# Run sums kept in PSUM, the weighted sum moved into a branch, and the rest of an FFN spread over the next attention

## The chip, the cores and the metric

The kernel is one program on one core of a Trainium2 chip. The core has TensorE (PE, with its weight loads listed as PEld), VectorE (DVE), ScalarE (ACT), GpSimd (POOL) and the DMA queues, of which SP and ACT issue plain transfers and POOL issues gathers by index. The metric is the device time of one execution in microseconds. The kernel before ran at a median of 6830.59 us over three runs (6827.94 to 6841.34).

## The reference

Four layers work on 6250 nodes with 256 features each, and each adds its result to `x`:

```python
x = x + gat(layernorm(x), src, dst, W, att_src, att_dst, bias)          # 4 heads of 64, 206,250 edges
x = x + moe(layernorm(x)[None], ...)                                     # 8 experts, the best 2 of each node
x = x + weighted_gnn(layernorm(x), src, dst, edge_weight, W1, b1, W2, b2)
x = x + gat_moe(layernorm(x)[None], ..., edge_index)                     # 4 heads of 4, routes to 4 experts
```

The change is about the third and the fourth. In the third, with `emb = layernorm(x)`:

```python
messages = edge_val[:, None] * embeddings[edge_src]
neighbor_emb = segment_sum(messages, edge_dst, n_nodes)
side_emb = (neighbor_emb + neighbor_emb * embeddings) @ W2.T + b2
out = leaky_relu(embeddings @ W1.T + b1 + side_emb, 0.2)
return out / max(norm(out), 1e-12)
```

In the fourth, an attention over a second list of 131,072 edges (its nodes are drawn from 0 to 8191, and those from 6250 on belong to no node here) gives every node a score for each of four experts; the best two weigh two of the four dense networks `gelu(x @ W1[e] + b1[e]) @ W2[e] + b2[e]`, which all run on all nodes.

## The kernel before

Nodes lie on 128 partitions in 49 blocks; `X` holds the features of all of them in SBUF throughout. An edge list sorted by target is cut into tiles of 128 edges, one edge a partition, and eight tiles (`Q = 8`) make a piece. One gather instruction of POOL fetches the 128 rows of one tile by a column of indices.

The stages follow each other: first attention (`gat_stream`, lines 1155 to 1388, over 1612 gathers), the FFN with eight experts (`routed_ffn`, loop from line 590), weighted sum (lines 1884 to 2033), second attention (`layer1_fast` at line 1685, which calls `gat_stream` again). Outside `tc.manual_schedule()` a planner orders the instructions of each engine; inside, they stay as written. The weighted sum's loop and both `gat_stream` loops are written out by hand.

Beside the first FFN run two generators, advanced four steps a tile of 256 rows (`next(beside, None)`): `sorted_edges` sorts the second edge list and checks it, `runs_of` (line 1524) prepares the weighted sum's indices `si_d`, weights `wab_d` and places `dab_d`. `runs_of` goes through two chunks of 128 pieces; its `turned` makes two times four transposes on PE, each set of four evicted by ScalarE.

The weighted sum first normalises `X` into a table in DRAM, `tab_ef` (lines 1885 to 1889), and then steps over 202 pieces. The edges of a piece lie in such a way that a partition holds eight consecutive edges, which belong to one target or two: two runs. `wab` has two weights for each edge, one for each run, of which one is zero. Step `s_` does, in this order:

- eight gathers for piece `s_` into `g1` (five buffers), line 234
- one piece of the second FFN's work, if there is any (`beside`)
- four matmuls `acc` for piece `s_ - 3` (line 2011), which add the run sums to their targets by one-hot matrices `oh`; after two pieces ScalarE takes the sum out (`kept`)
- another piece of FFN work
- the side steps of a finished block, one a step: `move` (shift to a block, PE), `side` (two transposes of two halves, with ScalarE's evictions between), `dense` (PE, then VectorE's `on`), `norm` (ScalarE and VectorE), `next_ln` (VectorE), `next_h` (transposes, then a small matmul and VectorE's `h`)
- `sum_runs(s_ - 2)`: ScalarE writes the first product of each run into SBUF, VectorE adds the 13 others (line 1922), and one instruction makes both one-hots from `ips`, a list of 0 to 127 in PSUM (line 1924)
- a third piece of FFN work

All engines take their instructions in order. `next_h` stores the second attention's rows to DRAM (`tab_1`, read by its gathers, and `ha_d`), and every four blocks it starts a group of the second FFN (`dense_ffn`, line 1616): pieces of eight matmuls into two PSUM buffers `pf`, each followed by a gelu or a copy on ScalarE and a store of `y1` to `y_d`. What is left of it when the loop ends runs in `while beside(): pass`. Then the program reads a flag that says whether the second list is in order, branches, and `layer1_fast` loads `si1`, `HN` (from `ha_d`), `dl1`, `il1` and starts its gathers; its step has five calls of its own `beside`, which do the weighted additions `put` (line 1756). The other branch sorts in a general way and isn't taken with these inputs.

PSUM has eight banks of 128 x 512 floats. The weighted sum uses all: `acc1` 2, `bacc1` 2, `pt` 1, `ips` 1, `pf` 2.

Of the kernel before, what the change touches and what calls it, by code (L numbers as in the profile page):

```python
# [20 lines left out]
F32 = mybir.dt.float32  # L21
BF = mybir.dt.bfloat16
I32 = mybir.dt.int32
# [9 lines left out]
P = 128  # L33
# [38 lines left out]
def tile_kernel(ctx, tc, src_ins, out):  # L72
# [1447 lines left out]
    def runs_of(s, sp, pp, si, wab, dab):  # L1520
# [19 lines left out]
        def turned(dst, src):  # L1540
            d, t = (a.rearrange("p (r j) -> p r j", j=Q) for a in (dst, src))
            for j0 in range(0, Q, 4):
                pt = pp.tile([P, 4, P], F32, name="pt_s")
                for j in range(4):
                    nc.tensor.transpose(pt[:, j], t[:, :, j0 + j], ident)
                nc.scalar.copy(d[:, :, j0:j0 + 4].rearrange("p r j -> p j r"), pt)

        for c in range(-(-npiece // P)):
# [4 lines left out]
            nc.vector.tensor_copy(b, a.bitcast(I32))  # L1553
            nc.vector.tensor_scalar(x, b, 0.0, float(N), op0=OP.is_lt, op1=OP.mult)
            nc.vector.tensor_add(b, b, x)
            nc.vector.tensor_scalar(b, b, 0.0, float(N - 1), op0=OP.max, op1=OP.min)
            yield
            y = room("B1")
            turned(y, b)
# [10 lines left out]
            turned(d, b)  # L1570
            yield
            load(w, I["edge_weight"], c, nr)
            wt = room("A0")
            turned(wt, w)
            yield
            d3 = d.rearrange("p (r j) -> p r j", j=Q)
            first = d3[:, :, 0:1].to_broadcast([P, P, Q])
            for k, op in enumerate((OP.is_equal, OP.not_equal)):
                m = room(("A1", "B1")[k])
                nc.vector.tensor_tensor(m.rearrange("p (r j) -> p r j", j=Q), d3, first, op=op)  # L1580
                nc.vector.tensor_mul(m, m, wt)
# [103 lines left out]
    def layer1_fast(s1, si1, dl1, il1, ha_d, tab_1, y_d):  # L1685
# [3 lines left out]
        with tc.tile_pool(name="g1f", bufs=1) as g1, tc.tile_pool(name="f1w", bufs=2) as fp:  # L1689
            si = g1.tile([P, s1.C * P], I32, name="si1s")  # L1690
            nc.sync.dma_start(si, si1)
            HN = g1.tile([P, NT, W1 + H1], F32, name="HN")
            nc.sync.dma_start(HN, ha_d)
# [75 lines left out]
            def beside():  # L1769
                if work:  # L1770
                    work.pop(0)()
                return bool(work)
# [5 lines left out]
    def fast(flag_s0, last_d, dl_d):  # L1778
# [104 lines left out]
        ha_d = dram.tile([P, NT, D1 + 2 * H1], F32, name="ha_d")  # L1883
        y_d = dram.tile([NT, P, C1, D], F32, name="y_d")
        with tc.tile_pool(name="n1e", bufs=2) as mp:
            for t0, n in chunks(NT, CH):
                em = mp.tile([P, CH, D], F32, name="em")
                layernorm(mp, em, X[:, t0:t0 + n, :], n)
                nc.sync.dma_start(tab_e[t0 * P:(t0 + n) * P].rearrange("(t p) d -> p t d", p=P), em[:, :n])
        with tc.tile_pool(name="n1f", bufs=1) as ep, tc.tile_pool(name="n1fw", bufs=2) as mp, \  # L1890
                tc.tile_pool(name="n1f_ps", bufs=1, space=PSUM) as pp, \
                tc.tile_pool(name="f1_ps", bufs=2, space=PSUM) as fpp:
            si = ep.tile([P, npiece * Q], I32, name="si8")
            nc.sync.dma_start(si, si_d)
            wab = ep.tile([P, 2, npiece * Q], F32, name="wab")
            nc.sync.dma_start(wab, wab_d.rearrange("k p t -> p k t"))
            dab = ep.tile([P, npiece * 2], F32, name="dab")
            nc.sync.dma_start(dab, dab_d)
            w12 = ep.tile([P, 2, KD, D], F32, name="w12")
            nc.sync.dma_start(w12[:, 0], I["L1_gnn_W1"].rearrange("(k p) f -> p k f", p=P))  # L1900
            nc.sync.dma_start(w12[:, 1], I["L1_gnn_W2"].rearrange("(k p) f -> p k f", p=P))
            bb = ep.tile([P, 2, D], F32, name="bb12")
            nc.sync.dma_start(bb[:, 0], rows(I["L1_gnn_b1"]))
            nc.sync.dma_start(bb[:, 1], rows(I["L1_gnn_b2"]))
            bias = ep.tile([P, D], F32, name="bias12")
            nc.vector.tensor_add(bias, bb[:, 0], bb[:, 1])
            wg = layer1_weights(ep)
            room, start, beside = dense_ffn(ep, mp, fpp, y_d)
            ips = place_iota(pp)
            acc, piece, runs, ems, sums_of = {}, {}, {}, {}, {}  # L1910

            def sum_runs(q):

                g = piece.pop(q)
                r = [mp.tile([P, D], F32, name=f"run{i}", bufs=3) for i in range(2)]
                for j in range(Q):
                    for i in range(min(2, j + 1)):
                        w = wab[:, i, q * Q + j:q * Q + j + 1]
                        if j == i:
                            nc.scalar.activation(r[i], g[:, j, :], AF.Copy, scale=w)  # L1920
                        else:
                            nc.vector.scalar_tensor_tensor(r[i], g[:, j, :], w, r[i], op0=OP.mult, op1=OP.add)  # L1922
                oh = mp.tile([P, 2, P], F32, name="oh", bufs=3)
                nc.vector.tensor_tensor(oh, ips[:, None, :P].to_broadcast([P, 2, P]),  # L1924
                                        dab[:, 2 * q:2 * q + 2, None].to_broadcast([P, 2, P]), op=OP.is_equal)
                runs[q] = r, oh

            def move(i, kept):

                whole = []  # L1930
                for b in range(NT):
                    of = s0.parts_of(b)
                    if i in of:
                        if b not in sums_of:
                            sums_of[b] = pp.tile([P, D], F32, name="bacc1", bufs=2)
                            ems[b] = mp.tile([P, D], F32, name="emb", bufs=3)
                            nc.sync.dma_start(ems[b], tab_e[b * P:(b + 1) * P])
                        nc.tensor.matmul(sums_of[b], shift_to(s0, i, b), kept, start=(i == of[0]), stop=(i == of[-1]))
                        if i == of[-1]:
                            whole.append(b)  # L1940
                return whole

            def side(b):
                sd = mp.tile([P, D], F32, name="sd_", bufs=2)
                nc.vector.scalar_tensor_tensor(sd, ems[b], 1.0, sums_of.pop(b), op0=OP.add, op1=OP.mult)
                eT = mp.tile([P, KD, P], F32, name="eT")
                transposed(pp, eT, ems.pop(b))
                sT = mp.tile([P, KD, P], F32, name="sT")
                transposed(pp, sT, sd)
                return eT, sT  # L1950

            def dense(b, eT, sT):
                po = pp.tile([P, KD, P], F32, name="pt").rearrange("p k e -> p (k e)")
                for k in range(KD):
                    nc.tensor.matmul(po, eT[:, k], w12[:, 0, k], start=(k == 0), stop=False)
                for k in range(KD):
                    nc.tensor.matmul(po, sT[:, k], w12[:, 1, k], start=False, stop=(k == KD - 1))
                o = mp.tile([P, D], F32, name="on")
                nc.vector.tensor_add(o, po, bias)
                nc.vector.scalar_tensor_tensor(o, o, 0.2, o, op0=OP.mult, op1=OP.max)  # L1960
                return o

            def norm(b, o):
                sq = mp.tile([P, D], F32, name="sq", bufs=1)
                ss = mp.tile([P, 1], F32, name="ss")
                nc.scalar.activation(sq, o, AF.Square, accum_out=ss)
                nc.scalar.activation(ss, ss, AF.Sqrt)
                nc.vector.tensor_scalar_max(ss, ss, 1e-12)
                nc.vector.reciprocal(ss, ss)
                nc.vector.scalar_tensor_tensor(X[:, b, :], o, ss, X[:, b, :], op0=OP.mult, op1=OP.add)  # L1970

            def next_ln(b):
                xl = mp.tile([P, 1, D], F32, name="xl1")
                layernorm(mp, xl, X[:, b:b + 1, :], 1)
                return xl

            def next_h(b, xl):
                o = b % GB * P
                xT = room(b // GB)[:, :, o:o + P]
                transposed(pp, xT, xl[:, 0, :])  # L1980
                ph = pp.tile([P, KD, P], F32, name="pt")[:, 0, :D1 + 2 * H1]
                for k in range(KD):
                    nc.tensor.matmul(ph, xT[:, k], wg[:, k], start=(k == 0), stop=(k == KD - 1))
                h = mp.tile([P, D1 + 2 * H1], F32, name="h1")
                nc.vector.tensor_copy(h, ph)
                nc.sync.dma_start(tab_1[b * P:(b + 1) * P], h[:, :D1 + H1])
                nc.sync.dma_start(ha_d[:, b, :], h)
                if b % GB == GB - 1 or b == NT - 1:
                    start(b // GB)

            chain = {side: dense, dense: norm, norm: next_ln, next_ln: next_h}


# [89 lines left out]
```

## Time and profile before

| what | us |
| --- | --- |
| median of three runs | 6830.59 |
| the profiled execution | 6821.2 |
| its span in the profile | 6819.3 |
| first attention, first to last gather | about 190 to 2240 |
| FFN with eight experts and its sum | about 2400 to 3400 |
| weighted sum, first to last gather | 3442 to 5623 |
| second attention, from its first gather | 5730 to 6819 |
| POOL busy | 4252.7 |
| VectorE busy | 4025.0 |
| TensorE busy | 3924.9 |
| ScalarE busy | 1166.6 |

A row of the groups names line, engine, operation and tile, then the count, the busy time in us, the mean of one in ns, and the engine's idle time just before these instructions with what ended it. A row in order of time has the start, the duration, the engine and, in brackets, how long the engine was idle before and for whom. A row of a stretch has its limits and length, then the busy time of PE, PEld, VectorE, ScalarE and POOL, PE's granted clock, the DMA share and GB/s.

### The profile page before, as it was taken

The numbers are of one execution on the slowest core, as the hardware profiler recorded it, in microseconds if no ns is written. First come the engines' busy times: TensorE is split into PE (matmuls) and PEld (weight loads), VectorE is DVE, ScalarE is ACT, GpSimd is POOL, SyncE is SP. The second block draws the span as 40 slices with busy tenths as digits, with TensorE's granted clock in tenths as the row PEclk, the third lists the DMA queues.
The fourth block names the chain that finished last, engine by engine and source line by source line (L and its number), as shares of the span: only waits on it lengthen the run. The fifth ranks groups of instructions, "written<-read, shape, count | busy, mean of one in ns | idle before, by whom it ended". The sixth has DMA issues, their size and how long they took to land.

```text
span 6819.3 us, 61938 instructions
## 1 busy us (share of the span) xinstructions
PE 3924.9 (58%) x17463; PEld 2934.8 (43%) x17463; DVE 4025.0 (59%) x9984; ACT 1166.6 (17%) x2834; POOL 4252.7 (62%) x4320
## 2 busy tenths in 40 slices
PE   4466665666666579998624566666666665111111
PEld 3344444444444468886513444444444443111111
DVE  5455555555555872443356565555566651788888
ACT  2000000000000112232112233323333332000000
POOL 0777777777777012332167777777777772777774
PEclk9677777777777589998856787778787887555555
DMA  4545555545554145556543444444444441223222
GB/s 135 139 137 139 138 138 139 138 138 138 138 137 128 45 128 194 186 185 206 163 152 105 110 115 113 112 112 113 112 114 114 113 113 53 64 66 66 68 66 56
DMA packets 502756, 822.99 MB, mean 121 GB/s; under 512 B 149744, under 2 KB 321987, under 8 KB 502370
## 3 DMA queue, kind: packets, MB, share of 16 engines
q0 software_dynamic: 190880, 462.26, 25.6%
q1 hardware_dynamic: 298854, 345.00, 16.5%
q10 hardware_dynamic: 12668, 11.68, 0.6%
q8 instruction: 141, 2.31, 0.1%
q14 instruction: 213, 1.74, 0.1%
HBM read 743.88 MB, written 77.89 MB: 121 GB/s over the span
## 4 chain that ended last, share of the span: by engine, by line
PE 26%; DVE 22%; POOL 19%; issue 15%; DMA 13%; ACT 4%; DVEq 0%; SPq 0%; another core or an unknown queue 0%; POOLq 0%; ACTq 0%
POOL g L1214 15%; DVE run L1922 7%; DMA g<-tab,si 7%; PE ph L601 5%; PE py L614 4%; POOL g L234 4%; PE acc L2011 4%; PE acc L1316 3%; PE pf L1654 2%; DMA g<-tab_1f,si1s 2%; DVE X L1756 2%; PE pf L1665 2%; DMA g<-tab_ef,si 2%; DVE g L1293 1%; PE pt L263 1%
## 5 line engine op out<-in xcount | busy, mean ns | idle before, releaser
L234 POOL DMA_INDIRECT g<-tab_ef,si x1616 | 1688.6, 1045 | 591.0 <-issue 437.0
L1214 POOL DMA_INDIRECT g<-tab,si x1612 | 1540.8, 956 | 494.3 <-issue 408.9
L1316 PE MATMUL acc<-g,oh 128*128 128x264 f32 x3224 | 1042.5, 488 | 338.8 <-DVE g L1293 333.9
L1922 DVE SCALAR_TENSOR_TENSOR run<-g,wab,run 128x256 f32<-128x256 f32 x2626 | 1088.8, 478 | 98.9 <-DMA g<-tab_ef,si 65.7
L1316 PEld LDWEIGHTS acc<-g,oh 128*128 128x128 f32 x3224 | 772.0, 247 | 560.4 <-DVE g L1293 394.5
L1214 POOL DMA_INDIRECT g<-tab_1f,si1s x787 | 770.1, 979 | 247.8 <-issue 213.3
L2011 PE MATMUL acc<-run,oh 128*128 128x256 f32 x808 | 336.9, 559 | 857.5 <-DVE oh L1924 857.2
L2011 PEld LDWEIGHTS acc<-run,oh 128*128 128x128 f32 x808 | 195.0, 265 | 993.4 <-DVE oh L1924 834.6
L1246 DVE TENSOR_TENSOR z<-g,nd 128x32 f32<-128x32 f32 (+1 forms) x301 | 57.7, 192 | 752.3 <-DMA g<-tab,si 654.2
L1293 DVE TENSOR_TENSOR g<-g,pe 128x2048 f32<-128x2048 f32 (+2 forms) x301 | 486.8, 1617 | 0.0
L1316 PE MATMUL acc<-s,oh 128*128 128x72 bf16 x1267 | 96.7, 251 | 601.4 <-DVE s L1298 601.4
L1654 PE MATMUL pf<-xt,w 128*128 128x512 f32 (+1 forms) x832 | 424.6, 650 | 1.5 <-ACT h L1659 1.0
L1665 PE MATMUL pf<-w,h 128*128 128x256 f32 x1568 | 413.9, 417 | 12.6 <-ACT h L1659 12.6
L601 PE MATMUL ph<-xe,w 128*128 128x256 f32 x1792 | 404.7, 382 | 0.0
L614 PE MATMUL py<-w,h 128*128 128x256 f32 x1792 | 400.7, 381 | 0.0
L577 POOL DMA_INDIRECT xg<-tab_x,gi x112 | 123.2, 1100 | 408.1 <-PE pt L586 322.4
L1665 PEld LDWEIGHTS pf<-w,h 128*128 128x128 f32 x1568 | 333.7, 214 | 86.8 <-ACT h L1659 17.5
L601 PEld LDWEIGHTS ph<-xe,w 128*128 128x128 f32 x1792 | 341.3, 192 | 45.6
L614 PEld LDWEIGHTS py<-w,h 128*128 128x128 f32 x1792 | 337.2, 191 | 43.3
L1316 PEld LDWEIGHTS <-oh 128*128 128x128 bf16 x1267 | 90.2, 134 | 605.2 <-issue 500.8
L1235 PEld LDWEIGHTS <-ot 128*128 128x128 bf16 x2879 | 116.1, 102 | 457.7 <-DVE ot L1224 403.3
L617 POOL DMA_INDIRECT tab_y<-y,so x112 | 118.6, 1059 | 296.6 <-DVE y L616 292.4
(486 smaller groups left out, 5689.4 us busy)
## 6 DMA issues: line engine op xcount, KB each, us to landing
w<-in_L_ffn_W SPq DMA_DIRECT2D x112, 1024.0 KB
db<-s_d SPq DMA_DIRECT2D x299, 256.0 KB
g<-tab_ef,si POOLq DMA_INDIRECT x1616
g<-tab,si POOLq DMA_INDIRECT x1612
y_d<-y SPq DMA_DIRECT2D x196, 128.0 KB
yb<-y_d SPq DMA_DIRECT2D x49, 512.0 KB
g<-tab_1f,si1s POOLq DMA_INDIRECT x787
yy<-tab_y SPq DMA_DIRECT2D x7, 1792.0 KB
```

The lines of the kernel that those rows point to most:

```text
L234: nc.gpsimd.indirect_dma_start(out=dst, out_offset=None, in_=table, in_offset=bass.IndirectOffsetOnAxis(ap=si[:, t:t + 1], axis=0))
L577: nc.gpsimd.indirect_dma_start(out=xg[:, i, :], out_offset=None, in_=tab_x, in_offset=bass.IndirectOffsetOnAxis(ap=gi[:, 2 * j + i:2 * j + ...
L601: nc.tensor.matmul(ph, w1[:, k, f * P:(f + 1) * P], xe[:, k, :], start=(k == 0), stop=(k == KD - 1))
L614: nc.tensor.matmul(py, hs[f][:, i * P:(i + 1) * P], w2[:, f, :], start=(f == 0), stop=(f == FC - 1))
L1214: nc.gpsimd.indirect_dma_start(out=g[:, j, :DH + H], out_offset=None, in_=tab, in_offset=bass.IndirectOffsetOnAxis(ap=si[:, t0 + j:t0 + j ...
L1293: nc.vector.tensor_mul(gh, gh, ps[i][:, o:o + n, :, None].to_broadcast([P, n, H, CD]))
L1316: nc.tensor.matmul(acc[b].rearrange("p s w -> p (s w)"), oh[:, t - a], m_, start=(t == lo), stop=(t == hi))
L1654: nc.tensor.matmul(ph[:, :n], w1[:, e, k, f * P:(f + 1) * P], xts[g][:, k, :n], start=(k == 0), stop=(k == KD - 1))
L1665: nc.tensor.matmul(py[:, :D], hs[g, e, f][:, j * P:(j + 1) * P], w2[:, e, f, :], start=(f == 0), stop=(f == FC - 1))
L1756: nc.vector.scalar_tensor_tensor(X[:, b, :], v[:, e, :], gates[:, j, e:e + 1], X[:, b, :], op0=OP.mult, op1=OP.add)
L1922: nc.vector.scalar_tensor_tensor(r[i], g[:, j, :], w, r[i], op0=OP.mult, op1=OP.add)
L2011: nc.tensor.matmul(acc[i], oh[:, k], r[k], start=(q % 2 == 0 and k == 0), stop=(last and k == 1))
```

## The change

Four things are changed.

- `sum_runs` keeps both run sums of a piece in one PSUM bank, `at`, until the last term, which goes to SBUF. The first product of the first run is made by VectorE, that of the second run still by ScalarE. The one-hots come from `iota` in SBUF, an instruction each, since `ips` gives its bank to `at`. `run` and `kept1` have two buffers for three.
- The weighted sum becomes a function that runs inside the branch on the second list's flag. `HN` is a tile in SBUF that `next_h` fills, `ha_d` goes, and `si1` and the FFN's weights are loaded at the start of the branch.
- `while beside(): pass` goes. What is left of the second FFN runs in the second attention's calls of `beside`, ahead of the additions.
- `runs_of` has more yields: after each instruction over a whole chunk and after each set of four transposes.

```diff
@@ runs_of
                     nc.tensor.transpose(pt[:, j], t[:, :, j0 + j], ident)
                 nc.scalar.copy(d[:, :, j0:j0 + 4].rearrange("p r j -> p j r"), pt)
+                yield
...
             nc.vector.tensor_copy(b, a.bitcast(I32))
+            yield
             nc.vector.tensor_scalar(x, b, 0.0, float(N), op0=OP.is_lt, op1=OP.mult)
+            yield
             nc.vector.tensor_add(b, b, x)
+            yield
             nc.vector.tensor_scalar(b, b, 0.0, float(N - 1), op0=OP.max, op1=OP.min)
             yield
             y = room("B1")
-            turned(y, b)
+            yield from turned(y, b)
...
-            turned(d, b)
-            yield
+            yield from turned(d, b)
             load(w, I["edge_weight"], c, nr)
             wt = room("A0")
-            turned(wt, w)
-            yield
+            yield from turned(wt, w)
...
                 nc.vector.tensor_tensor(m.rearrange("p (r j) -> p r j", j=Q), d3, first, op=op)
+                yield
                 nc.vector.tensor_mul(m, m, wt)
@@ layer1_fast
-    def layer1_fast(s1, si1, dl1, il1, ha_d, tab_1, y_d):
+    def layer1_fast(s1, si, dl1, il1, HN, tab_1, y_d, rest):
...
-            si = g1.tile([P, s1.C * P], I32, name="si1s")
-            nc.sync.dma_start(si, si1)
-            HN = g1.tile([P, NT, W1 + H1], F32, name="HN")
-            nc.sync.dma_start(HN, ha_d)
...
             def beside():
-                if work:
+                if not rest() and work:
                     work.pop(0)()
                 return bool(work)
@@ sum_runs
-                r = [mp.tile([P, D], F32, name=f"run{i}", bufs=3) for i in range(2)]
+                    at = pp.tile([P, 2, D], F32, name="run")
+                    r = [mp.tile([P, D], F32, name=f"run{i}", bufs=2) for i in range(2)]
                 for j in range(Q):
                     for i in range(min(2, j + 1)):
                         w = wab[:, i, q * Q + j:q * Q + j + 1]
-                        if j == i:
-                            nc.scalar.activation(r[i], g[:, j, :], AF.Copy, scale=w)
-                        else:
-                            nc.vector.scalar_tensor_tensor(r[i], g[:, j, :], w, r[i], op0=OP.mult, op1=OP.add)
+                            if j == 0:
+                                nc.vector.tensor_scalar(at[:, i], g[:, j, :], w, None, op0=OP.mult)
+                            elif j == i:
+                                nc.scalar.activation(at[:, i], g[:, j, :], AF.Copy, scale=w)
+                            else:
+                                nc.vector.scalar_tensor_tensor(at[:, i] if j < Q - 1 else r[i], g[:, j, :], w, at[:, i],
+                                                               op0=OP.mult, op1=OP.add)
                 oh = mp.tile([P, 2, P], F32, name="oh", bufs=3)
-                nc.vector.tensor_tensor(oh, ips[:, None, :P].to_broadcast([P, 2, P]),
-                                        dab[:, 2 * q:2 * q + 2, None].to_broadcast([P, 2, P]), op=OP.is_equal)
+                    for i in range(2):
+                        nc.vector.tensor_scalar(oh[:, i], iota, dab[:, 2 * q + i:2 * q + i + 1], None, op0=OP.is_equal)
@@ next_h
-                h = mp.tile([P, D1 + 2 * H1], F32, name="h1")
-                nc.vector.tensor_copy(h, ph)
-                nc.sync.dma_start(tab_1[b * P:(b + 1) * P], h[:, :D1 + H1])
-                nc.sync.dma_start(ha_d[:, b, :], h)
+                    nc.vector.tensor_copy(HN[:, b, :], ph)
+                    nc.sync.dma_start(tab_1[b * P:(b + 1) * P], HN[:, b, :D1 + H1])
@@ after the loop over pieces, and the branch
-                while beside():
-                    pass
...
+        def with_ffn(then):
+            with tc.tile_pool(name="f1e", bufs=1) as ep, tc.tile_pool(name="f1o", bufs=2) as fp, \
+                    tc.tile_pool(name="f1_ps", bufs=2, space=PSUM) as fpp:
+                HN = ep.tile([P, NT, D1 + 2 * H1], F32, name="HN")
+                si = ep.tile([P, C1s * P], I32, name="si1s")
+                nc.sync.dma_start(si, si1)
+                room, start, beside = dense_ffn(ep, fp, fpp, y_d)
+                weighted_sum(room, start, beside, HN)
+                then(si, HN, beside)
...
         with tc.If(v1 == 1) as cmp1:
-            layer1_fast(s1, si1, dl1, il1, ha_d, tab_1, y_d)
+            with_ffn(lambda si, HN, rest: layer1_fast(s1, si, dl1, il1, HN, tab_1, y_d, rest))
```

## The prediction

> **What bounds the kernel now.** I read the groups first, then the waits, then the rows in order of time. The bound of a change is about 0.2% (14 us): less can't be told from none.
>
> The groups give the weighted sum's gathers, its run sums and its matmuls:
>
> ```profile
> L234 POOL DMA_INDIRECT g<-tab_ef,si x1616 | 1688.6, 1045 | 591.0 <-issue 437.0
> L1214 POOL DMA_INDIRECT g<-tab,si x1612 | 1540.8, 956 | 494.3 <-issue 408.9
> L1922 DVE SCALAR_TENSOR_TENSOR run<-g,wab,run 128x256 f32<-128x256 f32 x2626 | 1088.8, 478 | 98.9 <-DMA g<-tab_ef,si 65.7
> L2011 PE MATMUL acc<-run,oh 128*128 128x256 f32 x808 | 336.9, 559 | 857.5 <-DVE oh L1924 857.2
> ```
>
> POOL's idle time is 98.9 us before the first gather and 0.30 us before every other: it never waits for a buffer, so gathers set this stage (1688.6 + 492 = 2181 us). A gather here takes 1045 ns; over the first attention, the same instruction takes 956. The rows in order of time show where the difference comes from:
>
> ```profile
> 4499.84 4.03 DVE L1922 SCALAR_TENSOR_TENSOR run<-g,wab,run 128x256 f32<-128x256 f32 x10
> ...
> 4501.83 1.28 POOL L234 DMA_INDIRECT g<-tab_ef,si  x1 [0.30 <-issue]
> ...
> 4505.00 0.95 POOL L234 DMA_INDIRECT g<-tab_ef,si  x1 [0.30 <-issue]
> ```
>
> Beside the run sums (two SBUF inputs: a row of `g` and `run`) a gather can take 1.28 us; once they are over, 0.95. Now the consumer, VectorE, over one block:
>
> ```profile
> 4066.34 0.42 DVE L1924 TENSOR_TENSOR oh<-ips,dab 128x256 f32<-128x256 f32 x1
> ...
> 4073.17 0.18 DVE L1985 COPY h<-pt 128x24 f32<-128x24 f32 x1 [6.08 <-PE pt L1983]
> 4073.26 5.35 DVE L1922 SCALAR_TENSOR_TENSOR run<-g,wab,run 128x256 f32<-128x256 f32 x13
> 4078.54 0.41 DVE L1924 TENSOR_TENSOR oh<-ips,dab 128x256 f32<-128x256 f32 x1
> 4084.48 0.42 DVE L1959 TENSOR_TENSOR on<-pt,bias 128x256 f32<-128x256 f32 x1 [5.53 <-PE pt L1957]
> ...
> 4090.55 0.41 DVE L1924 TENSOR_TENSOR oh<-ips,dab 128x256 f32<-128x256 f32 x1
> ...
> 4109.23 0.41 DVE L1924 TENSOR_TENSOR oh<-ips,dab 128x256 f32<-128x256 f32 x1
> ```
>
> Four pieces, that is about one block of 128 nodes, in 42.9 us, and no row among them waits for a gather; a piece takes 10.7 though its run sums take 5.35, because VectorE waits for PE in between. The loop is serial: run sums, one-hots, PE's `acc`, FFN and side matmuls, VectorE's side step, next run sums. Over the stage the first one-hot starts at 3473.2 and the last at 5626.83: 2153.6 us, 10.71 a piece. VectorE's waits for gathers (65.7 directly, 25.8 through ScalarE's run; 93.1 by the rows) are all the slack: without them the consumer needs 2060.5 us. **Two chains within 5% of each other**: whoever shortens one by lengthening the other must sum both.
>
> **1. Run sums in PSUM: the gathers.** With `at` in PSUM an instruction has one SBUF tensor left. The row for that is the first attention, whose big multiply reads `pe` from PSUM: 956 ns. So 1616 x (956 + 304) = 2036 us, 145 less. The other end is no gain at all (2181), if the operand is not the cause.
>
> **2. Run sums in PSUM: the consumer.** Per piece:
> - Term j = 0 moves from ScalarE to VectorE, 478 ns by L1922's row, and the next instruction reads its result; dependent rows (L1756 in the second attention) start 0.52 us apart, independent ones 0.40. Plus 0.52.
> - Second run's first product stays on ScalarE, now in the same PSUM bank as the first run. Halves of one bank are handed over one by one in this trace, though the halves are disjoint:
>
> ```profile
> 3342.28 0.27 ACT L1094 COPY ips<-iota 128x128 f32<-128x128 f32 x1 [6.88 <-DVE y L616]
> 3342.58 0.29 DVE L1095 TENSOR_SCALAR ips<-iota 128x128 f32<-128x128 f32 x1 [0.39 <-ACT ips L1094]
> ...
> 1000.57 0.20 ACT L1285 ACTIVATE g<-zt 128x32 f32<-128x32 f32 x1 [0.26 <-DVE g L1286]
> 1000.80 0.19 DVE L1286 TENSOR_TENSOR g<-zt,il 128x32 f32<-128x32 f32 x1 [0.26 <-ACT g L1285]
> ```
>
>  So VectorE's second instruction ends, ScalarE starts 0.03 later, takes 0.49 (L1920: 491 to 498 ns; evictions of this size take 0.37, a lower end), VectorE resumes 0.03 later; the old dependent gap of 0.04 falls away: plus 0.51. Its other end is 0, if it isn't handed over. Behind ScalarE's wait stand gelu and the `y` copies; PE's `pf` buffers need them, but PE idles 857 us for the one-hots (the group of `acc`) and can take that.
> - One-hots: two tensor_scalar from SBUF (L549: 279 ns each, 0.08 overlapped) for one of 413: plus 0.07.
> - 13 other instructions: a PSUM operand costs nothing by the rows (L1959 reads PSUM, 424 ns; L1860 reads SBUF, 424); the destination neither (L1095 into PSUM, 0.29). I take 0. The upper end is that neighbours in one bank also wait for each other, 0.52 for 0.40 on 11 of them: plus 1.3. A lower end below 0 is nothing I can place: L1945, with PSUM input and no pointer, is 0.02 shorter than L1861; 13 x 0.02 = 0.3 us a piece.
>
>  Sum 1.10 us; 201 x 1.10 = 221; the consumer needs 2282 and is the bound, 128 more than 2153.6. What is late next: gathers, now waiting for g's five buffers. Smaller buffer counts (`run`, `kept1`: 2) cost nothing: their readers are one step behind.
>
> [...]
>
> **3. FFN's rest beside the second attention.** Between the last one-hot (5626.83) and the next gather (5730.40) lie 103.6 us, 61 of them FFN alone:
>
> ```profile
> 5662.00:5723.00 61.00, 60.34 (x261) 44.87 (x259) 0.00 (x0) 20.19 (x46) 0.18 (x1) 1.00 0.13 42
> ...
> 5730.40 0.96 POOL L1214 DMA_INDIRECT g<-tab_1f,si1s  x1 [7.39 <-DMA vec<-in_L_ffn_ln_gamma]
> ```
>
> `si1` and HN are then in SBUF already (their loads, 5.4 us, and the 49 stores to `ha_d` on SP go). The last `tab_1` store is issued at 5661.4; with some 3 us to land and 3 of setup the first gather starts near 5667: minus 63. About 50 FFN items move into the first 10 steps, 5 a step. PE has 19% to do there; 5 x 1.7 = 8.5 us a step fit in a piece of 10.2. At half clock they are 17, a lag that nine g buffers take for three steps. I take plus 5, range 0 to 30. SP's `db` loads queue behind `y_d` stores that wait for ScalarE; they are issued two steps ahead, which covers it.
>
> **4. Weighted sum inside the branch.** The branch itself is about 1 us (flag at 65.62, SP's next load at 66.70). The layernorm can no longer fill VectorE's gaps in the sum over experts before it: two chunks, 7 us. ScalarE's queue gets the FFN's weight loads ahead of the layernorm's roots; these held it from 3436.4 to 3456.2. SP gets one `si1` load. Plus 15 (7 to 25).
>
> **5. More yields in the list's preparation.** In the first FFN, bound by PE, tiles of 14.25 us stretch to as much as 38 while transposes wait (12.4 us for the casts, 9.4 for edge weights), about 50 us in all. The steps now spread over 8.5 tiles in place of 4, with 4.5 tiles left. The wait for edge weights stays in one step. Minus 20 (0 to 40).
>
> **Sum.** 6821.2 (span 6819.3 and 1.9 around it; the median of the runs is 6830.6, 0.14% above) + 128 - 63 + 5 + 15 - 20 = **6886 us**.
>
> **Rivals.**
> - *The handover is hidden* (faster): ScalarE writes while VectorE adds. Consumer +0.59: 2179, +26; with -63 for the rest 6784. It decides at 0.78 us a piece (93 + 63 over 201). For: the halves are disjoint. Against: both pairs of rows above.
> - *Sum no longer than before* (faster): gathers and consumer meet at 2061: -93 - 63 = 6665. [...] Against: VectorE has an instruction more.
> - *Neighbours in one bank wait* (slower): +2.4 us a piece, 2543: 7147.
> - *The gathers don't get shorter*: 2181 stays under 2282, so nothing changes in mine; in the second rival it leaves the stage at 2181 and the whole at 6821 - 63 = 6758.
>
> **Numbers.** Mine 0.46, hidden handover 0.24, no longer sum 0.14, neighbours wait 0.11, others 0.05. The side terms spread mine by about 40 us, so of its 0.46 some 0.38 are slower, 0.04 same, 0.04 faster; the hidden handover gives 0.22 faster and 0.02 same, the third rival 0.11 slower, the others 0.04 slower and 0.01 faster. Range 6645 to 7010: it leaves out the waiting neighbours and some of the others. Slower 0.53, same 0.06, faster 0.41.
>
> **What would show it.** Right: gathers near 0.96 with POOL waiting for run sums; ScalarE's run idle behind VectorE, VectorE behind ScalarE, in every piece; one-hots 11.3 us apart; first gather of the second attention 40 us after the last one-hot. Wrong: POOL still without waits and one-hots 10.2 apart.

## The result, and the profile after

The changed kernel takes 7086.2 us in the median of four runs (7082.1 to 7091.4). Against the kernel before that is a ratio of 1.0372, with a 95% interval of 1.0354 to 1.0390. The prediction said 6886 and 6645 to 7010: the sign was right, the size was not, and the time lies outside the range. The experiments below were measured in four later sets of runs, each with the kernel before beside it, whose median was 7995, 6864, 7913 and 6849 us in turn; every ratio is to the kernel before of the same set.

The profiled execution has a span of 7089.6 us. Cut at the same events as the span before, it shows where the time came from:

| stretch | before | after | difference | predicted |
| --- | --- | --- | --- | --- |
| start to the start of the last `y` of the first FFN (yields) | 3341.8 | 3328.4 | -13.4 | -20 |
| from there to the first gather of the weighted sum (branch, start) | 100.5 | 112.0 | +11.5 | +15 |
| first gather to the end of the last one-hot (weighted sum) | 2184.9 | 2523.7 | +338.8 | +128 |
| from there to the first gather of the second attention | 103.2 | 37.7 | -65.5 | -63 |
| second attention | 1088.9 | 1087.8 | -1.1 | +5 |

Four of the five rows lie within 7 us of their terms; the whole miss is the weighted sum. The groups of the kernel after (busy time in us and mean of one in ns, then idle time just before and what ended most of it):

```profile
L234 POOL DMA_INDIRECT g<-tab_ef,si x1616 | 1528.7, 946 | 1054.8 <-issue 1022.2
L1214 POOL DMA_INDIRECT g<-tab,si x1612 | 1542.1, 957 | 494.1 <-issue 411.6
L1923 DVE SCALAR_TENSOR_TENSOR run<-g,wab,run 128x256 f32<-128x256 f32 x2626 | 1264.7, 488 | 211.7 <-ACT run L1921 111.8
L2011 PE MATMUL acc<-run,oh 128*128 128x256 f32 x808 | 337.0, 559 | 1102.7 <-DVE oh L1927 1102.7
```

The gathers did get shorter, 1045 to 946 ns, as forecast. But POOL's idle time rose from 591 to 1055 us. Of that, 0.30 us before each gather (485 us) is there in both kernels, and 110 us stand before the first gather (99 in the kernel before). The other 460 us or so are waits for a free buffer `g`, which the profile puts down as "issue": they come before the first gather of a piece, and in 125 pieces that gather starts about 0.74 us after the last addition that reads the buffer it is to fill. One of VectorE's additions is only 10 ns longer (478 to 488), yet together they are busy for 176 us more (1264.7 to 1088.8): they overlap less. The rows of VectorE and ScalarE in order of time, over one step:

```profile
4514.82 0.18 DVE L1986 COPY HN<-pt 128x24 f32<-128x24 f32 x1 [5.59 <-PE pt L1985]
4514.92 0.48 DVE L1919 TENSOR_SCALAR run<-g,wab 128x256 f32<-128x256 f32 x1
4515.43 0.49 DVE L1923 SCALAR_TENSOR_TENSOR run<-g,wab,run 128x256 f32<-128x256 f32 x1
4515.95 0.48 ACT L1921 ACTIVATE run<-g,wab 128x256 f32<-128x256 f32 x1 [2.27 <-DVE run L1923]
4516.47 6.12 DVE L1923 SCALAR_TENSOR_TENSOR run<-g,wab,run 128x256 f32<-128x256 f32 x12 [0.55 <-ACT run L1921]
4522.50 0.48 DVE L1927 TENSOR_SCALAR oh<-iota,dab 128x128 f32<-128x128 f32 x2
4528.22 0.42 DVE L1961 TENSOR_TENSOR on<-pt,bias 128x256 f32<-128x256 f32 x1 [5.24 <-PE pt L1959]
```

The last two of the twelve additions in a row of their own:

```profile
4521.72 0.87 DVE L1923 SCALAR_TENSOR_TENSOR run<-g,wab,run 128x256 f32<-128x256 f32 x2
```

Three things are to be read here. From 4515.43 VectorE stops until ScalarE has written its product: that is the handover of the bank, and it costs 1.04 us between two starts where 0.52 would be the next start. Then twelve additions take 6.12 us. From the first of them to the eleventh there are (4521.72 - 4516.47) / 10 = 0.525 us from start to start; only the last follows after 0.40. Before, thirteen took 5.35 us: 0.51 from the first to the second, which reads the first's result, and 0.40 between all others. And the two one-hots end 0.48 us after the first starts, with the next instruction starting after 0.39 where nothing is waited for; the one instruction before took 0.41. So the run sums take 7.6 us a piece where they took 5.3, and the wait for PE behind them is about as long as it was (5.24 us here, 5.53 at the same instruction before). The rows of POOL:

```profile
4518.61 0.94 POOL L234 DMA_INDIRECT g<-tab_ef,si  x1 [0.30 <-issue]
4523.33 0.94 POOL L234 DMA_INDIRECT g<-tab_ef,si  x1 [3.77 <-issue]
```

POOL, which never waited before, now stops between pieces. The one-hots are 12.48 us apart over the stage (2507.5 us for 201 steps), 10.71 before, 10.25 without the waits for gathers.

Theory to test: the additions of the two runs wait for one another because both runs lie in one PSUM bank (bank theory). Its rival: an addition onto PSUM needs that time whatever stands beside it (operand theory). The expectations call the spacing 0.51, its mean with the last pair. Behind both stands a second question, why 2.2 us of VectorE a piece became 2.2 us of the stage.

### The profile page after: what moved, and what is told of

Its sections match the earlier page's. It is cut to its first block, busy times and chain, and to the rows that moved or that the text cites. A ratio compares the mean times of both kernels' runs of the same rounds, so it can differ in the third digit from the quotient of the medians.

```text
span 7089.6 us, 62263 instructions
## 1 busy us (share of the span) xinstructions
PE 3990.0 (56%) x17463; PEld 2965.4 (42%) x17463; DVE 4310.0 (61%) x10387; ACT 1088.0 (15%) x2633; POOL 4094.6 (58%) x4320
## 5 line engine op out<-in xcount | busy, mean ns | idle before, releaser
L234 POOL DMA_INDIRECT g<-tab_ef,si x1616 | 1528.7, 946 | 1054.8 <-issue 1022.2
L1923 DVE SCALAR_TENSOR_TENSOR run<-g,wab,run 128x256 f32<-128x256 f32 x2626 | 1264.7, 488 | 211.7 <-ACT run L1921 111.8
L1316 PE MATMUL acc<-g,oh 128*128 128x264 f32 x3224 | 1047.0, 490 | 338.8 <-DVE g L1293 334.1
L1668 PE MATMUL pf<-w,h 128*128 128x256 f32 x1568 | 450.9, 444 | 39.2 <-ACT h L1662 28.4
L1657 PE MATMUL pf<-xt,w 128*128 128x512 f32 (+1 forms) x832 | 452.5, 682 | 29.1 <-ACT h L1662 18.1
L1668 PEld LDWEIGHTS pf<-w,h 128*128 128x128 f32 x1568 | 353.9, 228 | 126.9 <-ACT h L1662 33.7
L604 ACT ACTIVATE h<-ph,pa 128x256 f32<-128x256 f32 x448 | 211.9, 473 | 440.9 <-PE ph L601 440.6
```

What stands on the lines that cost most here:

```text
L234: nc.gpsimd.indirect_dma_start(out=dst, out_offset=None, in_=table, in_offset=bass.IndirectOffsetOnAxis(ap=si[:, t:t + 1], axis=0))
L604: nc.scalar.activation(h, ph, AF.Gelu, bias=pa[:, f:f + 1])
L1316: nc.tensor.matmul(acc[b].rearrange("p s w -> p (s w)"), oh[:, t - a], m_, start=(t == lo), stop=(t == hi))
L1657: nc.tensor.matmul(ph[:, :n], w1[:, e, k, f * P:(f + 1) * P], xts[g][:, k, :n], start=(k == 0), stop=(k == KD - 1))
L1668: nc.tensor.matmul(py[:, :D], hs[g, e, f][:, j * P:(j + 1) * P], w2[:, e, f, :], start=(f == 0), stop=(f == FC - 1))
L1923: nc.vector.scalar_tensor_tensor(at[:, i] if j < Q - 1 else r[i], g[:, j, :], w, at[:, i], op0=OP.mult, op1=OP.add)
```

## Experiments: bank or operand

Four kernels, the changed one among them, differ in where the run sums stand. The three new ones were first measured in the set in which the kernel before took 7995 us. All its traces show long waits, in stages that no kernel changes too, whose end the profile gives to no instruction of this core (`remote`): 907 us before ScalarE's `kept` of the first attention in one of them, none in the traces with 6830 to 6864 us. From that set only the spacing inside VectorE's sums and the gathers' durations are read. The two banks and, further below, the old run sums were measured again in the set with 6864; the total times expected of the other two kernels stay untested.

**Each run in a bank of its own.** `acc1` gives up its second buffer for it.

```diff
-                    at = pp.tile([P, 2, D], F32, name="run")
+                    at = [pp.tile([P, D], F32, name=f"at{i}") for i in range(2)]
...
-                                nc.vector.tensor_scalar(at[:, i], g[:, j, :], w, None, op0=OP.mult)
+                                nc.vector.tensor_scalar(at[i], g[:, j, :], w, None, op0=OP.mult)
...
-                            acc[i] = pp.tile([P, D], F32, name="acc1", bufs=2)
+                            acc[i] = pp.tile([P, D], F32, name="acc1", bufs=1)
```

> The changed kernel with each run in a PSUM bank of its own (acc1 gives one up). Bank theory (the two runs' instructions wait for each other because they lie in one bank): the additions come 0.40 us apart in place of 0.51, ScalarE's product falls beside VectorE's second instruction; a piece loses 1.8 us, 12.48 to 10.7, the stage 361: 6725, gathers stay at 0.95. Operand theory (an addition onto PSUM needs 0.51 whatever its neighbour): only ScalarE's 0.51 goes, 103 us in all: 6983.

> The two banks again. Bank theory: a piece at 10.7 us, 6725, or 0.985 of the kernel before; operand theory: 6983, 1.022.

Against 7995.2 us it took 8152.8, a ratio of 1.020 (1.0185 to 1.0221); against 6864.1 it took 6745.2, a ratio of 0.982 (0.9806 to 0.9838). The rows of VectorE of the second:

```profile
4508.16 0.18 DVE L1986 COPY HN<-pt 128x24 f32<-128x24 f32 x1 [7.34 <-PE pt L1985]
4508.26 0.48 DVE L1919 TENSOR_SCALAR at<-g,wab 128x256 f32<-128x256 f32 x1
4508.77 4.54 DVE L1923 SCALAR_TENSOR_TENSOR at<-g,wab,at 128x256 f32<-128x256 f32 x11
4513.22 0.87 DVE L1923 SCALAR_TENSOR_TENSOR run<-g,wab,at 128x256 f32<-128x256 f32 x2
4514.00 0.48 DVE L1927 TENSOR_SCALAR oh<-iota,dab 128x128 f32<-128x128 f32 x2
```

Eleven additions onto PSUM take 4.54 us: 0.525 from the first to the second, which reads the first's result, and 0.39 between the others, as in SBUF (0.40). VectorE no longer waits for ScalarE's product. First gather to last one-hot takes 2185.5 us in place of 2523.7: -338, with 361 expected. The operand theory falls. The 23 us that the stage lacks against the expectation are the 20 by which 6745 stands over 6725.

**Both runs as halves of one SBUF tile.**

```diff
-                    at = pp.tile([P, 2, D], F32, name="run")
-                    r = [mp.tile([P, D], F32, name=f"run{i}", bufs=2) for i in range(2)]
+                    rr = mp.tile([P, 2, D], F32, name="run", bufs=2)
+                    at, r = rr, [rr[:, i] for i in range(2)]
```

> The changed kernel with both runs as two halves of one SBUF tile, first products as changed (VectorE, ScalarE). Both theories have the additions 0.40 apart here if halves of an SBUF tile aren't handed over, sums of 5.9 us a piece; a theory that it is the shared tile and not the bank has them 0.51 apart, about as slow as the changed kernel. Gathers: if the second SBUF input makes them long, 1.045 us and 2181 for the stage: 6750 to 6770; if not, 0.95 and 6725.

Measured 7956.2 us, 0.995 (0.9934 to 0.9972) of the kernel before of that set. Halves of one SBUF tile aren't handed over: thirteen additions in 5.36 us, as in the kernel before (5.35).

```profile
5003.78 5.36 DVE L1923 SCALAR_TENSOR_TENSOR run<-g,wab,run 128x256 f32<-128x256 f32 x13
5009.06 0.48 DVE L1927 TENSOR_SCALAR oh<-iota,dab 128x128 f32<-128x128 f32 x2
```

**The first run in a PSUM bank, the second in SBUF.**

```diff
-                    at = pp.tile([P, 2, D], F32, name="run")
+                    at = [pp.tile([P, D], F32, name="run"), r[1]]
```

> The changed kernel with the first run in a PSUM bank and the second in SBUF. Bank theory: neighbours share nothing, 0.40 apart, sums of 5.9 us a piece: 6725 to 6740. Operand theory: 0.51 and 0.40 in turn, sums of 6.5 us, a piece 11.3: 6850. Gathers: half of the additions have two SBUF inputs, so about 1.00 us, between 0.95 and 1.045.

Measured 8022.3 us, 1.004 (1.0024 to 1.0064). Thirteen additions in 5.34 us, 0.39 to 0.40 apart, although every other one is onto PSUM: neither the tile nor the memory sets the 0.525, the common bank does.

The packed trace says how the bank does it. Each addition that starts 0.525 us after its neighbour waits for a semaphore that VectorE's own instructions raise, and starts 0.035 us after the neighbour's end, as an addition does in every kernel when it reads the neighbour's result. With a bank for each run the additions have waits for the same semaphore, but they start 0.09 us before the neighbour's end, so these are for an instruction further back. In the changed kernel the last addition of a piece carries no such wait in any of the 202 pieces, and it starts 0.40 us after a neighbour that reads the same bank. So the traces point to waits that stand in the program. Whether additions without them would be as fast when the neighbour also writes into the bank no run shows.

The two kernels also show the gathers' price, whose mean goes with the share of additions that have two SBUF inputs. Their groups, first of the kernel with both runs in SBUF, then of the one with a run in each:

```profile
L234 POOL DMA_INDIRECT g<-tab_ef,si x1616 | 1645.9, 1018 | 998.4 <-issue 916.7
```

```profile
L234 POOL DMA_INDIRECT g<-tab_ef,si x1616 | 1588.3, 983 | 1094.5 <-issue 963.0
```

All additions with two SBUF inputs: 1018 ns (1045 in the kernel before). Half of them: 983. None: 946 in the changed kernel, 947 with the banks apart. Counted over only those gathers that run beside the run sums for more than 0.5 us, the means are 1119 (1138 in the kernel before), 1032 and 946 to 947; beside an idle VectorE a gather takes 945 to 946 in all these kernels.

**The handover alone.** The second run's first product moves to VectorE; one bank as in the changed kernel.

```diff
-                            if j == 0:
+                            if j == i:
                                 nc.vector.tensor_scalar(at[:, i], g[:, j, :], w, None, op0=OP.mult)
-                            elif j == i:
-                                nc.scalar.activation(at[:, i], g[:, j, :], AF.Copy, scale=w)
```

> The changed kernel with the first product of the second run on VectorE too, so nothing is handed to ScalarE inside the bank. Term as sized (handover 0.51 beyond the instruction): ScalarE's 0.55 us becomes VectorE's own 0.51, at most 0.1 us a piece, 0 to 20 us less than the changed kernel: 1.034 to 1.037 of the kernel before. If the two handovers hide more (ScalarE late behind its copies), 50 us or more less: below 1.03.

Measured 7098.9 us against 6864.1, 1.034 (1.0321 to 1.0355). The ratio is at the lower edge of what was expected, but the stage tells the other sign: first gather to last one-hot takes 2537.6 us, 14 longer than with ScalarE's product. The two were measured in different sets, and 14 us is less than the sets differ by (6830 and 6864 for the kernel before); what holds is that in this order the handover costs about as much as an instruction of VectorE's own.

## Experiments: the other parts

**Run sums as before, everything else as changed.** `run` keeps two buffers, the one-hots stay two instructions.

```diff
-                    at = pp.tile([P, 2, D], F32, name="run")
...
-                            if j == 0:
-                                nc.vector.tensor_scalar(at[:, i], g[:, j, :], w, None, op0=OP.mult)
-                            elif j == i:
-                                nc.scalar.activation(at[:, i], g[:, j, :], AF.Copy, scale=w)
+                            if j == i:
+                                nc.scalar.activation(r[i], g[:, j, :], AF.Copy, scale=w)
                             else:
-                                nc.vector.scalar_tensor_tensor(at[:, i] if j < Q - 1 else r[i], g[:, j, :], w, at[:, i],
-                                                               op0=OP.mult, op1=OP.add)
+                                nc.vector.scalar_tensor_tensor(r[i], g[:, j, :], w, r[i], op0=OP.mult, op1=OP.add)
```

> The changed kernel with the run sums and their first products as before, in SBUF (run with two buffers); branch, FFN's rest and yields as changed, one-hots still two instructions from SBUF. If the run sums are the whole loss, the other three parts keep what the stages showed (-13 yields, +11 branch, -65 FFN's rest, -1 second attention): 6830 - 68 = 6762, gathers back at 1.045 us and POOL without waits again. If another part hides a loss in the longer stage, it stands above 6800.

> Run sums and first products as before, the other three parts as changed, again: the stages give -68 us, 6762, 0.990 of the kernel before, with the weighted sum's gathers back at 1.045 us; a hidden loss in the other parts would show as 0.995 or more.

Against 7995.2 us it took 7962.1, 0.995 (0.9930 to 0.9969), the value that would have spoken for a hidden loss; but the traces of that set are longer in nearly every stage. Against 6864.1 it took 6760.0, 0.984 (0.9826 to 0.9860), and its stretches show no loss: -12 to the last `y`, 2195.9 for the weighted sum (gathers 1052 ns, POOL again without waits), 40.4 to the next gather, 1088.3 for the second attention. The time expected, 6762, came; the ratio is lower because the kernel before took 6864 in that set, 34 more than beside the changed kernel. Where those 34 lie no trace shows.

Put beside the two banks (6745), this says what the run sums in PSUM alone are worth in this loop, even with the bank wait gone: 0.2%, which is not clear of noise (0.982 and 0.984, each within 0.002). The gathers become 100 ns shorter, but then VectorE's loop is the bound, at 2185 us.

**The FFN's rest ahead of the second attention again**, on top of the kernel with the old run sums:

```diff
                 weighted_sum(room, start, beside, HN)
+                while beside():
+                    pass
                 then(si, HN, beside)
```

> Run sums as before, the other parts as changed, but the FFN's rest runs ahead of the second attention again. If its overlap is worth what the stages showed (65 us from last one-hot to first gather, of which 61 are the FFN alone), 0.984 + 0.009 = 0.993 of the kernel before; if the second attention only pays for it elsewhere, under 0.987.

> Run sums as before, FFN's rest ahead of the second attention, again: 0.984 + 0.009 = 0.993 of the kernel before if the overlap is worth its 61 us; under 0.987 if the second attention pays for it elsewhere.

Against 7912.8 us it took 7889.0, 0.997 (0.9950 to 0.9983); against 6848.8 it took 6751.0, 0.985 (0.9824 to 0.9874), where the kernel without this edit has 0.984. So the edit costs nothing that these runs show, and 0.993 was wrong. First the row of the kernel before, then those of this kernel:

```profile
5722.82 0.19 POOL L1137 IOTA s_nid<- 128x49 f32 x1 [99.78 <-PE pf L1665]
```

```profile
5659.59 0.18 POOL L1137 IOTA s_nid<- 128x49 f32 x1 [34.16 <-PE pt L263]
5667.07 0.96 POOL L1214 DMA_INDIRECT g<-tab_1f,si1s  x1 [7.30 <-DMA vec<-in_L_ffn_ln_gamma]
...
5688.35 7.07 PE L1668 MATMUL pf<-w,h 128*128 128x256 f32 x32
...
5706.04 0.18 PE L1235 MATMUL pd<-NB,ot 128*128 128x24 bf16 x1
5706.26 1.16 PE L1657 MATMUL pf<-xt,w 128*128 128x128 f32 x8
```

Before, POOL's first instruction of the second attention waited 99.8 us for PE's last FFN matmul. Here the FFN's rest stands ahead of the attention in the program's text as well, yet POOL waits only for a transposition of the weighted sum, and gathers run from 5667 beside FFN matmuls. From 5706 PE even takes the attention's matmuls (`pd`) between those of the FFN: the loop now stands outside `manual_schedule`, where the planner is free to order the instructions. So this edit did not take the overlap away, and it can't say what the overlap is worth. What it shows is that the 65 us don't need the FFN's pieces in the second attention's calls of `beside`; they come with the weighted sum and the FFN standing inside the branch. Whether that is because no branch lies between any more, because the FFN's loop is no longer bound to its written order, or because the attention no longer takes over the FFN's buffers, these runs don't separate.

## Experiments: why the loss is the stage's

VectorE is busy for 1579 of the weighted sum's 2524 us. If its 2.2 us more a piece became the stage's, the theory is that the order is the reason: one-hots, PE's `acc`, the side matmuls, VectorE's side step and the next run sums follow each other.

**Run sums ahead of the side steps**, one bank, ScalarE's product as changed:

```diff
+                        if 0 <= s_ - 2 < npiece:
+                            sum_runs(s_ - 2)
                         for f, b, args in after.pop(s_, []):
...
-                        if 0 <= s_ - 2 < npiece:
-                            sum_runs(s_ - 2)
                         beside()
```

> The changed kernel with one move: sum_runs(s_ - 2) stands ahead of the side steps, not behind them; the run sums stay in one PSUM bank. If the loss is worth 12.48 us a piece only because VectorE's sums (7.6 us), PE's matmuls and the side step follow each other, VectorE now sums while PE works, a piece needs some 9.5 us of VectorE and the gathers (0.95 + 0.30, 8 times, 10.0 us) set the stage: about 2045 in place of 2523, in all 0.93 of the kernel before or 6610 to 6650. If PE or ScalarE carry the piece, it stays over 1.01 of the kernel before.

Measured 6863.0 us against 6864.1, a ratio of 1.000 (0.999 to 1.001). The expectation's 6610 to 6650 us are 0.93 of the changed kernel, not of the kernel before, of which they are 0.97. The stage falls from 2523.7 to 2295.9, half of what was expected. The rows of VectorE and of ScalarE and PE of this kernel show what holds it now:

```profile
4507.62 0.49 DVE L1923 SCALAR_TENSOR_TENSOR run<-g,wab,run 128x256 f32<-128x256 f32 x1
4513.84 6.12 DVE L1923 SCALAR_TENSOR_TENSOR run<-g,wab,run 128x256 f32<-128x256 f32 x12 [5.73 <-ACT run L1921]
```

```profile
4510.60 0.69 ACT L1662 ACTIVATE h<-pf,bt 128x512 f32<-128x512 f32 x1 [4.14 <-PE pf L1657]
4512.75 0.69 ACT L1662 ACTIVATE h<-pf,bt 128x512 f32<-128x512 f32 x1 [1.47 <-PE pf L1657]
4513.34 0.47 ACT L1921 ACTIVATE run<-g,wab 128x256 f32<-128x256 f32 x1
```

```profile
4554.47 0.66 PE L263 MATMUL pt<-ident,sd__25149 128*128 128x128 f32 x2 [6.20 <-DVE sd__25149 L1947]
```

ScalarE's product now stands in its queue behind two gelus that wait for PE, so VectorE waits up to 7 us for one product (435 us over the stage, 112 in the changed kernel). And PE waits 6 to 9 us for `sd`, which VectorE makes behind the run sums. The handover that cost about as much as an instruction in one order costs more than ten times as much at worst in another.

**Both mended**: first products on VectorE, `sd` ahead of the run sums, these ahead of the other side steps. One kernel keeps the one bank, the other has a bank for each run.

```diff
-                            if j == 0:
+                            if j == i:
                                 nc.vector.tensor_scalar(at[:, i], g[:, j, :], w, None, op0=OP.mult)
-                            elif j == i:
-                                nc.scalar.activation(at[:, i], g[:, j, :], AF.Copy, scale=w)
...
-                def side(b):
+                def scaled(b):
                     sd = mp.tile([P, D], F32, name="sd_", bufs=2)
                     nc.vector.scalar_tensor_tensor(sd, ems[b], 1.0, sums_of.pop(b), op0=OP.add, op1=OP.mult)
+                    return sd
+
+                def side(b, sd):
...
-                        for f, b, args in after.pop(s_, []):
+                        due = [(f, b, (scaled(b),) if f is side else args) for f, b, args in after.pop(s_, [])]
+                        if 0 <= s_ - 2 < npiece:
+                            sum_runs(s_ - 2)
+                        for f, b, args in due:
...
-                        if 0 <= s_ - 2 < npiece:
-                            sum_runs(s_ - 2)
```

> The changed kernel, both runs still in one PSUM bank, with three moves: both first products on VectorE, sd made ahead of the run sums, the run sums ahead of the other side steps. What held the kernel with the sums moved alone was VectorE behind ScalarE's product (395 us) and sd behind the sums; both are gone. VectorE then has 15 x 0.51 + 0.4 + about 1.0 us a piece, 9.1 to 9.6, under the gathers' 10.0: first gather to last one-hot about 2045 in place of 2523, 0.967 of the kernel before (6610 where that is 6830). If PE's chain through ScalarE's copies holds the piece, 0.985 or more.

> One bank, VectorE's chain freed, again. If the gathers bound the piece: 0.967 of the kernel before; if PE's chain through ScalarE's copies holds it, 0.985 or more.

> The same with a bank for each run: VectorE 15 x 0.41 + 0.4 + 1.0, 7.6 us a piece. Theory that the gathers are the bound once the loop's order is mended: the same time as with one bank, 0.967, within 0.004. If VectorE still bounds the piece, the 1.6 us show: up to 0.02 less.

> A bank for each run, VectorE's chain freed, again. If the gathers bound the piece with one bank already: within 0.004 of the one-bank kernel; if VectorE's 1.6 us still count, up to 0.02 less.

Against 7912.8 us they took 7978.7 and 7988.4, ratios of 1.009 (1.0061 to 1.0127) and 1.011 (1.0074 to 1.0140); the traces of this set show the same `remote` waits, and nothing more is read from it than that the two are alike. Against 6848.8 us they took 6598.4 and 6597.2, ratios of 0.9635 (0.9613 to 0.9656) and 0.9631 (0.9610 to 0.9653). There both are faster than the kernel before and than the changed one. VectorE's additions and the waits of POOL between 3500 and 5400 us in the one-bank kernel:

```profile
L1921 DVE SCALAR_TENSOR_TENSOR run<-g,wab,run 128x256 f32<-128x256 f32 x2626 | 1264.5, 488 | 268.5 <-DMA g<-tab_ef,si 195.1
```

```profile
POOL g L234 <- issue: 425.3, 1396, 0.3
POOL g L234 <- DVE run L1921: 34.4, 113, 0.3
POOL g L234 <- DMA g<-tab_ef,si: 2.4, 8, 0.3
```

No wait of POOL's there is longer than the usual 0.30 us, and VectorE waits for gathers. The stage takes 2028.4 us for 1616 x (0.948 + 0.30) = 2017: the gathers are the bound, and the 1.6 us a piece that the second bank takes off VectorE don't count. The bank wait is as long here as in the changed kernel (488 ns of one, 0.525 apart where the gathers are in time), and it costs nothing. What each of the three moves is worth by itself was not measured.

## Why the prediction was wrong, point by point

- *What bounds the kernel* (two chains within 5%): right. The old run sums leave 2196 us with gathers as bound, the two banks 2185 with the loop as bound, and taking time off both gives 2028.
- *Part 1, gathers to 956 ns*: right, 946. Its cause, the second SBUF input, held: 1018 to 1072, 983 and 946 to 951 as all, half or none of the additions have it. The 404 one-hots, tensor_scalar instructions between SBUF tiles, don't lengthen them: the gathers of the stage take 946 ns in the mean, and 949 the 69 of them that run beside a one-hot for more than 0.2 us.
- *Part 2, term j = 0 and handover, 0.52 and 0.51*: right in this order of the loop, by the rows at 4514.92 to 4516.47 (0.51 and 1.04 - 0.52). *One-hots, 0.07*: nothing, 0.39 for 0.41.
- ***Part 2, "13 other instructions ... I take 0"*: this is the step that failed.** Ten spacings a piece grew from 0.396 to 0.525 us, 1.29 us a piece. The upper end stood there almost to the digit, 0.52 for 0.40 on 11, plus 1.3. I passed over it because L1959 and L1860 (424 ns each), L1095 and L549 (0.29 and 0.28 us) show that PSUM costs nothing as source or destination. That is right, the two banks show it again (485 ns of one, 0.39 apart), but it answers another question: those rows have no neighbour in their bank. The row that was nearest, the handover of `ips` and `g` between engines within one bank (the second starts 0.03 us after the first ends), I used for ScalarE's product and not for VectorE's own neighbours. With 1.29 in place of 0 and 0 in place of 0.07 the sum is 2.32 a piece; measured are 2.224 (12.475 - 10.251), and the 0.1 between them isn't taken apart. 201 x 2.224 - 93 = 354, less 15 for a first one-hot that came earlier: the 339 of the table.
- *The rival "neighbours in one bank wait"*: this is what happened, 7147 against 7086, given 0.11 and left outside the range. *The hidden handover* fell.
- *Part 3, -63*: the number right (-65.5), and the FFN's rest does run beside the second attention. That it takes the second attention's calls of `beside` is not so: with the loop ahead of the attention again, inside the branch, the gain stayed. The lag that I charged with 5 us did not come (-1.1).
- *Parts 4 and 5, +15 and -20*: +11.5 and -13.4, by the stretches; neither was run alone.
- *Why neighbours in one bank wait* is open. With a bank for each run additions onto PSUM start 0.39 us apart, in SBUF 0.40; in one bank VectorE stops for ScalarE's product at disjoint halves (1.04 us between two starts), and its own additions start 0.525 us apart. The semaphores in the traces point to the program's own ordering; taking that wait away alone was not tried.

## What to carry to other kernels

In a loop like this one, two accumulators that take turns belong in two PSUM banks: in one, each instruction starts only when its neighbour is done, 0.525 in place of 0.39 us, and another engine's product there stops the first for 0.5 us or, behind gelus in its queue, for up to 7. Price an operand's memory and its neighbours apart, by rows that have the neighbours. And where an engine that is busy for 63% of a stage sets its length, look at the order before the instructions: three moves brought 6.9% (7086 to 6598 us, in different sets of runs), nearly twice what the whole change had lost.

## What the runs showed of the hardware that was not expected

- VectorE's additions onto disjoint halves of one PSUM bank start 0.525 us apart, each behind a semaphore for its neighbour's end; in two banks they start 0.39 apart, on halves of one SBUF tile 0.40.
- A gather takes POOL 946 to 951 ns in the mean, 983, or 1018 to 1072, as none, half or all of VectorE's additions beside it read two SBUF tensors.
- The kernel before took 7995 and 7913 us in two sets of runs, up to 17% more than the 6830 to 6864 of the other three. What the waits named `remote` in those traces wait for the profile doesn't show, and since the record gives one chip number to the sets with 6864 and 7913, they can't be put down to a chip. Even the sign of the kernels with the mended order turned there (1.009 against 0.964).
